# Two transformer layers on one core: order of the work at eight places

## Chip, core and metric

One NeuronCore of a Trainium2 chip (trn2) runs the whole kernel. The metric is the device time of one execution in microseconds (us), as a median over runs. Engines are named as in the profile: PE is TensorE (PEld its weight loads), DVE is VectorE, ACT is ScalarE, POOL is GpSimd, SP is SyncE, which issues most of the DMAs.

## The reference

The input is x of shape [2, 512, 512]: two sequences of 512 tokens with 512 features. Two layers follow one another, each of an attention and a feed-forward part, with a residual addition and a LayerNorm after each part. Cut to what matters:

```python
# layer 0, attention: reads from a memory M (8 heads of 128x128) with a normaliser z
q   = elu(x @ Wq.T + bq) + 1              # only each fourth of 32 heads is used: 8
out = (q @ M) / (q . z + 1e-6)            # per head, repeated four times
x   = layernorm(x + out.reshape(...) @ Wo.T)

# layer 0, feed-forward, quantized: weights in {-1, 0, 1} * scale
xf    = x / 128
inter = silu(xf @ w_gate.T) * (xf @ w_up.T)                 # 1376 wide
iq    = trunc(clip(inter * 128, -128, 127)).astype(int8)
d     = iq @ w_down.T
x     = layernorm(x + trunc(clip(d * 128, -128, 127)))

# layer 1, attention: one head of 128, softmax
q, k, v = split(x @ Wqkv + bqkv)
x = layernorm(x + softmax(q @ k.T / sqrt(128)) @ v @ Wo + bo)

# layer 1, feed-forward in float32
x = layernorm(x + (silu(x @ w_gate.T) * (x @ w_up.T)) @ w_down.T)
```

## The kernel before

The tokens of a sequence are four tiles of 128 rows (t = 0 to 3), the features four blocks of 128 columns (k = 0 to 3), the inner width of the feed-forward parts eleven chunks (c = 0 to 10, the last of 96). x stays on the chip from the first load to the last store, normalised in place. The eight PSUM banks are handed round: a matmul group can begin when the engines that read the bank's earlier content are done.

The order of the work on an engine is that in which the program writes its calls, as far as a scheduler doesn't move an instruction forward; POOL's order is as written. Where the program wants an instruction behind another of the same engine, it says so with `tc.issue_after(step.ins)`. Each engine takes its instructions in that order.

The stages, in order of time:

- Head. `load_x(0)` (L74) issues four loads of x on SP. `rise` (L98) runs nine matmuls on a tile of ones. `transposed` (L105) turns x on PE, a block k per bank, and copies each bank to SBUF, even blocks on ACT (L124), odd ones on DVE (L126). `queries(b, xt, h)` (L318) multiplies by Wq and applies elu + 1: two ACT passes, one on DVE (L331).
- The four parts of Wo of a head are summed by `sum_weights` on DVE or POOL (L345, L347), and `fold` multiplies them into the memory. The buffers of Wo are six, so SP can issue a later load only when an earlier tile was summed. `largest` (L169, L174) takes the maximum of the gate and up weights, from which their scale follows; `check_up` compares each chunk with its ternary form on ACT (L398) and DVE.
- Attention reads. `read(b, t, ...)` (L357) does eight matmuls per tile (L366) and adds the results to x on DVE (L388) and, for three heads, through ACT and POOL; `norm_a0` normalises the tile of the read before. After the seventh read (i = 6), `split(0)` (L249) turns sequence 0 into four blocks and cuts each into a high part (ACT, L259) and a low part (DVE, L260), all four in a row.
- Up projection of layer 0. `up(b, c)` (L515) does 32 matmuls (L522) into two banks, silu on ACT (L535), the product, the cut and the int8 parts on DVE and ACT. The order is `up(0, 0..2)`, `split(1)`, `up(1, 0..2)`, then both sequences by turns. `to_divide` names the ternary weights that ACT makes after each call. `check_down` (L561) compares w_down with its ternary form, through POOL (L400).
- Down projection of layer 0. `f0_down(i)` (L605) starts tile i (22 matmuls, L575), reads it out (`scaled`, L592), adds the tile before (`added`) with its LayerNorm statistics (L132, L134, and POOL's root, L140 and L141), and normalises the one before that (`layernorm_apply`, L146), which is tied behind the last addition of the tile before. Two tiles are started before `up(1, 10)`, the last of the up projection.
- Layer 1, attention. `scores(b)` (L777) makes four banks of scores and, for each, the row maximum (L784, L785) in the same loop; `exponentials` (L789) follows. `values`, `output` and `attended` follow. `norm_a1(b, t)` (L856) takes statistics, then POOL makes the root and the offset (L140 to L842), then ACT applies it (L843).
- Layer 1, feed-forward. Each operand is split into three parts, so that each product is three fast matmuls. `split_rows(b, room)` (L873) does this for x: transposes (L879), a copy (L885), a cut and `row_parts`. `up1` multiplies (L937) and adds up (`sum_up`, L947 and L948). `down1(b, t, got, cuts)` (L1000) does the down projection and the last LayerNorm; the last tile runs in two halves of 256 columns (`cuts` = 2), whose normalisations stand behind one another on DVE (L146), with one store on SP and one on ACT (L1033).

Of the kernel before, what the change touches and what calls it, by code (L numbers as in the profile page):

```python
# [36 lines left out]
def kernel(  # L37
# [36 lines left out]
    def load_x(b):  # L74
        for t in range(NT):
            x = xp.tile([P, HID], F32, tag="x", name=f"x_{b}_{t}")
            nc.sync.dma_start(x, x_in[b, ts(t, P), :])
            xs[b].append(x)
# [19 lines left out]
    rise = psum("rise")  # L98
    for _ in range(9):
        nc.tensor.matmul(rise[:, :P], ones, ones, start=True, stop=True)  # L100
# [3 lines left out]

    def transposed(rows, name, by_tile=False):  # L105

        xt = xtp.tile([P, NK, S], F32, tag="xt", name=f"xt_{name}")
        pts = {}

        def turn(k, t):  # L110
            if k not in pts:
                pts[k] = psum(f"pt_{name}_{k}")
            nc.tensor.transpose(pts[k][:, ts(t, P)], rows[t][:, ts(k, P)], ident)

        if by_tile:
            for t in range(NT):
                for k in range(NK):
                    turn(k, t)
        for k in range(NK):
            if not by_tile:  # L120
                for t in range(NT):
                    turn(k, t)
            if k % 2 == 0:
                copies.append(nc.scalar.copy(xt[:, k, :], pts[k]))  # L124
            else:
                copies.append(nc.vector.tensor_copy(xt[:, k, :], pts[k]))  # L126
        return xt

    def layernorm_stats(row, name):

        st = small.tile([P, 6], F32, tag="st", name=f"st_{name}")
        nc.vector.bn_stats(st, row)  # L132
        mv = small.tile([P, 2], F32, tag="mv", name=f"mv_{name}", bufs=8)
        nc.vector.bn_aggr(mv, st)  # L134
        return root(mv, name)
# [113 lines left out]
    def split(b):  # L249

        hi = xtp.tile([P, NK, S], F32, tag="xt", name=f"xh_{b}").bitcast(F32R)
        los = [pair_tile(f"xl_{b}_{i}").bitcast(F32R) for i in range(2)]
        his = [hi[:, k, :] for k in range(NK)]
        los = [los[k // 2][:, k % 2, :] for k in range(NK)]
        for k in range(NK):
            pt = psum(f"pt_f0{b}_{k}")
            for t in range(NT):
                nc.tensor.transpose(pt[:, ts(t, P)], xs[b][t][:, ts(k, P)], ident)
            nc.scalar.copy(his[k], pt)  # L259
            nc.vector.tensor_sub(los[k], pt, his[k].bitcast(F32))  # L260
        return his + los

# [11 lines left out]
    with tc.tile_pool(name="a0w", bufs=1) as a0w, tc.tile_pool(name="a0", bufs=2) as a0:  # L274
# [42 lines left out]

        def queries(b, xt, h):  # L318

            pq = psum(f"pq_{b}_{h}")  # L320
            for k in range(NK):
                nc.tensor.matmul(  # L322
                    pq, wq[h][:, k, :], xt[:, k, :], start=(k == 0), stop=(k == NK - 1)
                )

# [91 lines left out]
        qs = [[], []]  # L417
        xt = transposed(xs[0], "a00", by_tile=True)
        for h in range(NH):
            queries(0, xt, h)  # L420
            if h == 4:
# [55 lines left out]
        for i, (b, t) in enumerate(order):  # L477
# [7 lines left out]
            if i in (3, 4, 5):  # L485
                for a in range(2):
                    divided(i - 3, a)
            elif i == 6:
                x2.append(split(0))
        norm_a0(len(order) - 1, steps)  # L490
# [16 lines left out]
    with tc.tile_pool(name="f0", bufs=2) as f0:  # L507
# [6 lines left out]

        def up(b, c):  # L515
            n = CHUNKS[c][1]
# [17 lines left out]
            sg = fp.tile([P, S], F32, tag="sg", name=f"sg_f0{b}_{c}")  # L534
            nc.scalar.activation(sg[:n], pp[0][:n], AF.Silu, scale=silu_scale[:n])  # L535
            y = f0.tile([P, S], F32, tag="y", name=f"y_f0{b}_{c}")
# [50 lines left out]

        pds, ys, stats, behind = {}, {}, {}, {}

        def scaled(i):  # L590
            y = f0.tile([P, HID], F32, tag="y", name=f"yd_{i}")
            nc.scalar.activation(y, pds[i], AF.Copy, scale=down_scale)  # L592
            cut_to_12(y)
            ys[i] = y

        def added(i):
# [4 lines left out]
            nc.vector.scalar_tensor_tensor(x, tb, 128.0, x, ALU.min, ALU.subtract)  # L601
            behind[i] = nc.vector.scalar_tensor_tensor(x, x, -1.0, ta, ALU.mult, ALU.add)
            stats[i] = layernorm_stats(x, f"f0_{i}")

        def f0_down(i):  # L605
# [5 lines left out]
            if 0 <= i - 2 < len(order):  # L611

                b, t = order[i - 2]
                with tc.issue_after(behind[min(i, len(order)) - 1].ins):
                    layernorm_apply(xs[b][t], xs[b][t], stats[i - 2])

        for c in range(3):
            up(0, c)
        x2.append(split(1))
        to_divide.insert(2, None)  # L620
        for c in range(3):
            up(1, c)
        for c in range(3, 8):
            step = up(0, c)
            if c == 3:
                with tc.issue_after(step.ins):
                    mx_d = largest([wds[0]], "down")
            elif c == 4:
                sc_d, inv_d = scales(top_d, "down")
            up(1, c)  # L630
            if c == 3:
                top_d = over_partitions(mx_d, "down")
            else:
                for i in range(2 * c - 8, 2 * c - 6):
                    check_down(i)
        up(0, 8)
        check_down(8)
        check_down(9)
# [10 lines left out]
        for i in range(2):  # L649
            f0_down(i)  # L650
        up(1, 10)
        for i in range(2, len(order) - 1):
# [123 lines left out]

    def scores(b):  # L777
        qt, kt, _ = qkv[b]
        got = []
        for t in range(NT):  # L780
            p = psum(f"psc_{b}_{t}")
            nc.tensor.matmul(p, qt[:, ts(t, P)], kt, start=True, stop=True)
            mx = small.tile([P, 1], F32, tag="mx", name=f"mx_{b}_{t}", bufs=8)
            nc.vector.reduce_max(mx, p, AX.X)  # L784
            scaled_max = nc.vector.tensor_scalar_mul(mx, mx, -scale)  # L785
            got.append((p, mx))
        return got, scaled_max

# [16 lines left out]

    got, scaled_max = scores(0)
    got1, scaled_max = scores(1)
    exponentials(0, got)
    for b in range(B):
        for t in range(NT):  # L810
            nc.gpsimd.tensor_add(xs[b][t], xs[b][t], bo)
    pt0 = transposed(probs[0][0], "p0")
    table(AF.Silu, exponentials(1, got1, {1: copies[-4], 2: copies[-2]}))
    with tc.issue_after(scaled_max.ins):
# [58 lines left out]
    def split_rows(b, room):  # L873

        parts, moved = [], []
        for k in range(NK):
# [3 lines left out]
            if b or k:  # L880
# [5 lines left out]
                pt = rows  # L886
            m = cut(pt, S, f"x{b}_{k}")
            parts.append(room[3 * k : 3 * k + 3])
# [14 lines left out]
    x3[0], done = split_rows(0, rooms[0])  # L903
    with tc.issue_after(done.ins):
        for t in range(NT):
            norm_a1(1, t)

# [92 lines left out]
    def down1(b, t, got, cuts):  # L1000
# [22 lines left out]
        nc.vector.bn_aggr(mv, st)  # L1023
        stats = root(mv, f"f1_{b}_{t}")
        if cuts == 1:
            scalar_norm(x, stats, f"f1_{b}_{t}")
            nc.sync.dma_start(out[b, ts(t, P), :], x)
        else:
            for i in range(cuts):
                cols = slice(i * w, (i + 1) * w)  # L1030
                layernorm_apply(x[:, cols], x[:, cols], stats)
                eng = nc.scalar if i else nc.sync
# [92 lines left out]
```

## Time and profile before

| | |
|---|---|
| Median of 3 runs | 488.73 us (488.49 to 488.89) |
| The profiled execution's own time | 488.72 us |
| Its span in the trace | 486.9 us |
| Mean granted TensorE clock | 0.997 |
| PE busy / idle in the span | 473.4 / 13.5 us |
| First matmul of the warm-up, first transpose | 1.16, 5.16 us |
| First query matmul | 8.13 us |
| End of statistics of the last tile, last issue of a store | 482.4, 484.1 us |

How to read it: the span runs from the first to the last recorded instruction; the profiled execution's own time is 1.8 us longer. A line of the timeline has the start and the length in us, the engine, the line of the program, the operation, output and inputs, their shapes, and how many instructions are merged into it; in brackets stands how long the engine was idle before it, and which instruction of which engine ended that. A matmul's end is modelled, so the starts say more than the ends. A float32 matmul has two records.

### The profile page before, as it was taken

The page shows a single profiled execution, that of the slowest core. Times are in us where ns is not written, and L with a number is a line of the kernel's source. Part 1 is how long each engine was busy: PE and PEld are TensorE (multiplying, and loading weights), DVE is VectorE, ACT ScalarE, POOL GpSimd, SP SyncE. Part 2 cuts the span into 40 slices and gives each one's busy share as a digit, 9 for nine tenths or more (in the row PEclk, how much of TensorE's full clock was granted, in tenths as well). Part 3 has the DMA queues.
Part 4 walks back from the last instruction along what each step waited for, and adds up shares of the span by engine and source line. Part 5 has one row for each costly group of instructions (what it writes and reads, how often), then busy time and mean ns, then how long its engine had stood idle before and what let it go on. Part 6 is the DMA issues. An engine that isn't in the chain of part 4 may idle for free.

```text
span 486.9 us, 5812 instructions
## 1 busy us (share of the span) xinstructions
PE 473.4 (97%) x1885; PEld 328.6 (67%) x1885; DVE 352.9 (72%) x682; ACT 275.0 (56%) x513; POOL 115.2 (24%) x155
## 2 busy tenths in 40 slices
PE   8999999999999999999899999999999999999995
PEld 6454444434487788787666467788788888888885
DVE  1456677677675477754989989698876687999942
ACT  2344799555767666545835845776754566333310
POOL 0334102666520096000347032100000000023211
PEclk9999999999999999999999999999999999999998
DMA  8989800000052001131390000000000000000111
GB/s 295 389 314 339 319 1 1 0 0 1 2 160 74 1 3 45 45 90 34 119 370 4 1 0 2 0 2 0 1 0 0 1 1 1 0 22 24 43 45 43
DMA packets 13749, 33.99 MB, mean 70 GB/s; under 512 B 1872, under 2 KB 2768, under 8 KB 13712
## 3 DMA queue, kind: packets, MB, share of 16 engines
q1 hardware_dynamic: 13568, 33.37, 19.3%
q8 instruction: 22, 0.36, 0.3%
q14 instruction: 15, 0.12, 0.1%
q10 hardware_dynamic: 144, 0.13, 0.1%
HBM read 31.40 MB, written 2.10 MB: 69 GB/s over the span
## 4 chain that ended last, share of the span: by engine, by line
PE 58%; DVE 15%; ACT 8%; issue 4%; POOL 2%; POOLq 0%; DVEq 0%; ACTq 0%
PE pm L937 15%; PE pdm L1012 8%; PE pg_f L522 8%; PE pu_f L522 8%; PE pc L937 8%; PE pdc L1012 4%; DVE x L388 4%; ACT y L379 2%; ACT t L398 2%; PE po L847 1%; PE pot L830 1%; PE po L366 1%; DVE x L146 1%; PE pd_f L575 1%; DVE mx L784 1%
## 5 line engine op out<-in xcount | busy, mean ns | idle before, releaser
L366 PE MATMUL po<-mw,q 128*128 128x512 f32 x128 | 56.7, 597 | 1.2 <-DVE x L388 0.9
L322 PE MATMUL pq<-xt_a,wq 128*128 128x512 f32 x128 | 56.5, 593 | 0.3 <-ACT xt_a L124 0.3
L140 POOL TENSOR_TENSOR rstd_f<-mv_f,ln_eps 128x1 f32<-128x1 f32 x16 | 4.5, 283 | 193.3 <-DVE mv_f L1023 139.1
L366 PEld LDWEIGHTS po<-mw,q 128*128 128x128 f32 x128 | 23.2, 189 | 33.2 <-issue 18.9
L322 PEld LDWEIGHTS pq<-xt_a,wq 128*128 128x128 f32 x128 | 24.0, 190 | 29.6 <-issue 28.1
L937 PE MATMUL pm<-r,it_early 128*128 128x512 f32 x144 | 37.7, 392 | 0.4 <-ACT r L695 0.4
L937 PE MATMUL pm<-r,ugu 128*128 128x512 f32 (+1 forms) x144 | 36.8, 393 | 0.0
L937 PEld LDWEIGHTS pm<-r,it_early 128*128 128x128 f32 x144 | 26.9, 188 | 6.6 <-ACT r L695 0.7
L388 DVE SCALAR_TENSOR_TENSOR x<-po,den,x 128x511 f32<-128x511 f32 x40 | 29.8, 745 | 2.0
L937 PEld LDWEIGHTS pm<-r,ugu 128*128 128x128 f32 (+1 forms) x144 | 26.8, 186 | 6.3
L162 ACT ACTIVATE ta_f<-y_f,below_half 128x512 int8<-128x512 f32 (+1 forms) x22 | 15.9, 722 | 25.2 <-DVE y_f L152 24.9
L948 DVE SCALAR_TENSOR_TENSOR ev_q<-pm,ev_q 128x512 f32<-128x512 f32 (+1 forms) x28 | 19.2, 688 | 14.3 <-PE pm L937 14.0
L383 POOL TENSOR_TENSOR y<-y,y 128x511 f32<-128x511 f32 x16 | 20.3, 1270 | 32.1 <-ACT y L379 31.4
L400 POOL TENSOR_SCALAR td<-wd,inv_down 128x512 fp32r<-128x512 f32 (+1 forms) x11 | 19.5, 1790 | 30.3 <-DVE inv_down L196 30.3
L937 PE MATMUL pc<-r,ugu 128*128 128x512 f32 (+1 forms) x96 | 26.1, 394 | 0.0
L545 DVE SCALAR_TENSOR_TENSOR it_f<-tb_f,ta_f 128x512 fp32r<-128x512 int16 (+1 forms) x22 | 15.1, 688 | 15.1 <-ACT tb_f L163 15.1
L327 ACT ACTIVATE e<-pq,bq 128x512 f32<-128x512 f32 x16 | 11.1, 693 | 25.9 <-PE pq L322 25.9
L522 PE MATMUL pg_f<-xh,tu 128*128 128x512 f32 (+1 forms) x88 | 25.6, 406 | 0.1
L522 PE MATMUL pg_f<-xl,tu 128*128 128x512 f32 (+1 forms) x88 | 24.4, 395 | 0.1
L522 PE MATMUL pu_f<-xh,tu 128*128 128x512 f32 (+1 forms) x88 | 24.0, 394 | 0.0
L331 DVE SCALAR_TENSOR_TENSOR q<-e,r 128x512 f32<-128x512 f32 x16 | 13.8, 862 | 13.9 <-ACT r L329 13.9
L522 PE MATMUL pu_f<-xl,tu 128*128 128x512 f32 (+1 forms) x88 | 23.9, 393 | 0.0
(286 smaller groups left out, 1114.9 us busy)
## 6 DMA issues: line engine op xcount, KB each, us to landing
gu<-in_gu SPq DMA_DIRECT2D x20, 512.0 KB, 8.9
wo<-in_wo SPq DMA_DIRECT2D x16, 512.0 KB, 7.4
wd<-in_wd SPq DMA_DIRECT2D x20, 256.0 KB, 4.8
x<-in_x SPq DMA_DIRECT2D x8, 256.0 KB, 4.6
wq<-in_wq SPq DMA_DIRECT2D x8, 256.0 KB, 4.6
out<-x SPq DMA_DIRECT2D x7, 256.0 KB, 2.0
gu<-in_gu SPq DMA_DIRECT2D x2, 384.0 KB, 6.5
wqkv<-in_wqkv SPq DMA_DIRECT2D x1, 768.0 KB, 10.7
```

What stands on the lines that cost most here:

```text
L162: nc.scalar.activation(a[:n], y, AF.Relu, bias=below_half[:n])
L322: nc.tensor.matmul(pq, wq[h][:, k, :], xt[:, k, :], start=(k == 0), stop=(k == NK - 1))
L331: nc.vector.scalar_tensor_tensor(q, e, 1.0, r, ALU.min, ALU.add)
L366: nc.tensor.matmul(po, qs[b][h0 + j][:, ts(t, P)], mw[:, h0 + j, :], start=True, stop=True,)
L383: nc.gpsimd.tensor_add(ys[0][:, :LAST], ys[0][:, :LAST], y[:, :LAST])
L388: steps.append(nc.vector.scalar_tensor_tensor(x[:, :LAST], four[j][:, :LAST], d, x[:, :LAST], ALU.mult, ALU.add))
L400: eng.tensor_scalar(out, w, factor, None, ALU.mult)
L522: nc.tensor.matmul(pp[a][:n], t[:, a, i % NK, :n], x2[b][i], start=(i == 0), stop=(i == 2 * NK - 1),)
L545: nc.vector.scalar_tensor_tensor(it[:n], tb[:n], 128.0, ta[:n], ALU.min, ALU.subtract)
L937: nc.tensor.matmul(p[:n], w, x, start=(left[id(p)] == begun[id(p)]), stop=(left[id(p)] == 1))
L948: nc.vector.scalar_tensor_tensor(ev[:n], pm, MAIN, ev[:n], ALU.mult, ALU.add)
L1012: nc.tensor.matmul(p[:, :w], got[j // 4][1][kind][:n, j % 4], down_parts[j][kind][:, cols], start=(j == 0 and kind == kinds[0]), stop=(j = ...
```

## The change

Eight places are changed. (1) The four loads of sequence 0 go to SP and ACT by turns, the warm-up has eight matmuls, and the first transposes, their copies and the first query run in two halves of 256 tokens. (2) Two of the four blocks of `split(0)` follow the sixth read, two the seventh. (3) In the up projection, `up(0, 3)` follows the split of sequence 1, and sequence 0 stays a chunk further ahead. (4) The last silu is tied behind the read-out of the first two down tiles, and a tile's normalisation is tied behind the first statistics instruction of the next tile instead of behind its addition. (5) The last row maximum of sequence 1 stands behind a copy of the turned probabilities. (6) A cut of sequence 0's second block is tied behind the first block's last part. (7) The normalisation of sequence 1 after attention takes all four statistics first and applies on DVE. (8) In the last tile, the mean is subtracted on DVE beside the root on POOL, and the halves are multiplied by the root on DVE and ACT.

```diff
     def load_x(b):
...
-            nc.sync.dma_start(x, x_in[b, ts(t, P), :])
+            eng = nc.scalar if b == 0 and t % 2 else nc.sync
+            eng.dma_start(x, x_in[b, ts(t, P), :])
...
-    for _ in range(9):
+    for _ in range(8):
         nc.tensor.matmul(rise[:, :P], ones, ones, start=True, stop=True)
...
-    def transposed(rows, name, by_tile=False):
+    def transposed(rows, name, cuts=0):
...
+        def copy(k, at, i=0):
+            move = nc.vector.tensor_copy if k % 2 else nc.scalar.copy
+            copies.append(move(xt[:, k, at], pts[k, i][:, at]))
+
+        if cuts:
+            for i in range(cuts):
+                for t in range(i * NT // cuts, (i + 1) * NT // cuts):
+                    for k in range(NK):
+                        turn(k, t, i)
                 for k in range(NK):
-                    turn(k, t)
...
+                    copy(k, ts(i, S // cuts), i)
...
+    taken = {}
+
     def layernorm_stats(row, name):
...
-        nc.vector.bn_stats(st, row)
+        taken[name] = nc.vector.bn_stats(st, row)
...
     def split(b):
...
-        for k in range(NK):
+
+        def block(k):
             pt = psum(f"pt_f0{b}_{k}")
...
-        return his + los
+
+        return his + los, block
...
-        def queries(b, xt, h):
+        def queries(b, xt, h, cuts=1):
...
+            for i in range(cuts):
+                at = ts(i, S // cuts)
+                for k in range(NK):
+                    nc.tensor.matmul(
+                        pq[:, at], wq[h][:, k, :], xt[:, k, at],
+                        start=(k == 0), stop=(k == NK - 1),
+                    )
...
-        xt = transposed(xs[0], "a00", by_tile=True)
+        xt = transposed(xs[0], "a00", cuts=2)
         for h in range(NH):
-            queries(0, xt, h)
+            queries(0, xt, h, 1 if h else 2)
...
-            elif i == 6:
-                x2.append(split(0))
+            if i == 5:
+                parts, block = split(0)
+                x2.append(parts)
+            if i in (5, 6):
+                for k in range(2):
+                    block(2 * (i - 5) + k)
...
-        def up(b, c):
+        def up(b, c, behind=()):
...
-            nc.scalar.activation(sg[:n], pp[0][:n], AF.Silu, scale=silu_scale[:n])
+            with ExitStack() as tied:
+                for step in behind:
+                    tied.enter_context(tc.issue_after(step.ins))
+                nc.scalar.activation(sg[:n], pp[0][:n], AF.Silu, scale=silu_scale[:n])
...
-            nc.scalar.activation(y, pds[i], AF.Copy, scale=down_scale)
+            moved[i] = nc.scalar.activation(y, pds[i], AF.Copy, scale=down_scale)
...
-                with tc.issue_after(behind[min(i, len(order)) - 1].ins):
+                with tc.issue_after(taken[f"f0_{min(i, len(order)) - 1}"].ins):
                     layernorm_apply(xs[b][t], xs[b][t], stats[i - 2])
 
+        to_divide[2:2] = [None, None]
         for c in range(3):
             up(0, c)
-        x2.append(split(1))
-        to_divide.insert(2, None)
+        parts, block = split(1)
+        x2.append(parts)
+        for k in range(NK):
+            block(k)
+        step = up(0, 3)
+        with tc.issue_after(step.ins):
+            mx_d = largest([wds[0]], "down")
         for c in range(3):
             up(1, c)
-        for c in range(3, 8):
-            step = up(0, c)
-            if c == 3:
-                with tc.issue_after(step.ins):
-                    mx_d = largest([wds[0]], "down")
-            elif c == 4:
+        top_d = over_partitions(mx_d, "down")
+        for c in range(4, 8):
+            up(0, c)
+            if c == 4:
                 sc_d, inv_d = scales(top_d, "down")
-            up(1, c)
-            if c == 3:
-                top_d = over_partitions(mx_d, "down")
-            else:
-                for i in range(2 * c - 8, 2 * c - 6):
-                    check_down(i)
+            up(1, c - 1)
+            for i in range(2 * c - 8, 2 * c - 6):
+                check_down(i)
         up(0, 8)
+        up(1, 7)
         check_down(8)
...
-        up(1, 10)
+
+        up(1, 10, moved.values())
...
     def scores(b):
...
-            nc.vector.reduce_max(mx, p, AX.X)
-            scaled_max = nc.vector.tensor_scalar_mul(mx, mx, -scale)
-            got.append((p, mx))
-        return got, scaled_max
+            got.append((p, small.tile([P, 1], F32, tag="mx", name=f"mx_{b}_{t}", bufs=8)))
+
+        def maxima(tiles):
+            for t in tiles:
+                p, mx = got[t]
+                nc.vector.reduce_max(mx, p, AX.X)
+                done = nc.vector.tensor_scalar_mul(mx, mx, -scale)
+            return done
+
+        return got, maxima
...
-    got, scaled_max = scores(0)
-    got1, scaled_max = scores(1)
+    got, maxima = scores(0)
+    maxima(range(NT))
+    got1, maxima = scores(1)
+    maxima(range(NT - 1))
...
     pt0 = transposed(probs[0][0], "p0")
+    with tc.issue_after(copies[-3].ins):
+        scaled_max = maxima([NT - 1])
...
-            m = cut(pt, S, f"x{b}_{k}")
+            with ExitStack() as tied:
+                if b == 0 and k == 1:
+                    tied.enter_context(tc.issue_after(done.ins))
+                m = cut(pt, S, f"x{b}_{k}")
...
-    with tc.issue_after(done.ins):
-        for t in range(NT):
-            norm_a1(1, t)
+    stats1 = []
+    for t in range(NT):
+        with tc.issue_after(done.ins):
+            stats1.append(layernorm_stats(xs[1][t], f"a11_{t}"))
+    for t in range(NT):
+        with tc.issue_after(taken["a11_3"].ins):
+            layernorm_apply(xs[1][t], xs[1][t], stats1[t])
...
-        stats = root(mv, f"f1_{b}_{t}")
...
         else:
+            rstd = small.tile([P, 1], F32, tag="rstd", name=f"rstd_f1_{b}_{t}", bufs=8)
+            nc.vector.tensor_scalar(rstd, mv[:, 1:2], LN_EPS, None, ALU.add)
+            nc.gpsimd.tensor_tensor(rstd, rstd, minus_half, ALU.pow)
+            nc.vector.tensor_scalar(x, x, mv[:, 0:1], None, ALU.subtract)
+            nc.vector.tensor_scalar(x[:, :w], x[:, :w], rstd, None, ALU.mult)
+            nc.scalar.activation(x[:, w:], x[:, w:], AF.Copy, scale=rstd)
             for i in range(cuts):
                 cols = slice(i * w, (i + 1) * w)
-                layernorm_apply(x[:, cols], x[:, cols], stats)
```

## The prediction

> **What bounds the kernel now.** I read the busy table first, then the idle time of TensorE (PE) in the timeline, wherever one of its lines carries a wait. Here is the page's table and the chain that ended last:
>
> ```profile
> PE 473.4 (97%) x1885; PEld 328.6 (67%) x1885; DVE 352.9 (72%) x682; ACT 275.0 (56%) x513; POOL 115.2 (24%) x155
> PE 58%; DVE 15%; ACT 8%; issue 4%; POOL 2%; POOLq 0%; DVEq 0%; ACTq 0%
> ```
>
> PE is busy for 473.4 of 486.9 us, so only 13.5 us are idle, and the change removes no matmul but one. All it can win is PE's waits, its start and what follows its last matmul. The waits of the timeline (start, us, engine and line, operation; in brackets the idle time and who ended it):
>
> ```profile
> 8.13 2.41 PE L322 MATMUL pq<-xt_a,wq 128*128 128x512 f32 x5 [0.35 <-ACT xt_a L124]
> 125.46 1.12 PE L366 MATMUL po<-mw,q 128*128 128x512 f32 x2 [0.87 <-DVE x L388]
> 145.97 0.19 PEld L522 LDWEIGHTS pg_f<-xh,tu 128*128 128x128 f32 x1 [0.29 <-ACT xh L259]
> 222.35 0.69 ACT L535 ACTIVATE sg_f<-pg_f,silu_scale 96x512 f32<-96x512 f32 x1 [3.74 <-PE pg_f L522]
> 242.38 0.66 PE L113 MATMUL pt_a<-ident,x 128*128 128x128 f32 x4 [1.55 <-DVE x L146]
> 255.22 1.53 PE L113 MATMUL pt_a<-ident,x 128*128 128x128 f32 x12 [0.80 <-DVE x L146]
> 277.27 1.55 PE L830 MATMUL pot<-xt_p,v 128*128 128x512 f32 x3 [0.49 <-DVE xt_p L126]
> 307.51 1.64 PE L879 MATMUL pt_f<-ident,x 128*128 128x128 f32 x13 [1.04 <-ACT x L843]
> ```
>
> A matmul's recorded end reaches beyond the start of the next, so idle time understates a wait. I price a wait as start less previous start, less the usual step: 0.43 us (fp32, 512 columns), 0.23 (fp32r: eight in 1.86), 0.11 (128-column transpose at full clock). This gives 0.51 us at 8.13, 1.03 at 125.46 and 0.38 at 126.80, 1.77 in eight small pieces from 145.97 to 149.4, 1.71 at 242.38 and 0.51 at 243.38, 0.97 at 255.22, 0.66 at 277.27, 1.24 at 307.51. Together 8.8.
>
> The table by stretches (PE, PEld, DVE, ACT, POOL busy) warns where another engine has no room: ACT is full in 56 to 84, DVE nearly so in 310 to 330.
>
> ```profile
> 56.00:84.00 28.00, 27.93 (x66) 12.16 (x65) 20.26 (x50) 28.00 (x59) 2.53 (x2) 1.00 0.10 35
> 310.00:330.00 20.00, 20.00 (x89) 16.25 (x88) 19.60 (x38) 14.88 (x29) 1.08 (x2) 1.00 0.01 1
> ```
>
> And the end, after PE's last matmul:
>
> ```profile
> 482.46 0.19 POOL L140 TENSOR_TENSOR rstd_f<-mv_f,ln_eps 128x1 f32<-128x1 f32 x1 [5.72 <-DVE mv_f L1023]
> 482.73 0.57 POOL L141 TENSOR_TENSOR rstd_f<-rstd_f,minus_half 128x1 f32<-128x1 f32 x1
> 483.34 0.74 DVE L146 TENSOR_SCALAR x<-x,mv_f,rstd_f 128x256 f32<-128x256 f32 x2 [0.96 <-POOL rstd_f L141]
> 484.10 0.37 ACTq L1033 DMA_DIRECT2D out<-x  x1
> ```
>
> **What the Trainium skill says.** "PSUM — Partial Sum Buffer", section "Engine vs sequencer instructions": ScalarE, VectorE and GpSimdE take their queues strictly first in, first out. The trace agrees: ACT stood idle 3.74 us for the silu at 222.35 while the read-out queued behind it was ready by about 218. "TensorE: Matmul & The Clock Gate", Part 1: the array starts at half clock and gets full clock after about 3.4 us of steady work, in a free-running window. Here transposes step 0.21 us until 6.62 and 0.11 after, 5.5 us after the first matmul: longer, same pattern. "SBUF — State Buffer", section "SBUF: two separate sides": DVE and GpSimd share a port pair that one locks for an instruction. It agrees: a normalisation on DVE (L146) takes 0.55 us at 241.78 and 1.49 at 253.68, beside POOL's additions of bo. "DMA: Bandwidth & Descriptors", section "Issuing engines are not separate DMA queues": a second issuer saves only issue time. The first four loads of x take 1.81 us to issue on SP.
>
> **The change, part by part.** Times are those of before.
>
> 1. Head. One warm-up matmul less is two records of 0.213: transposes begin at 4.73, not 5.16. Eight of 16 are done by about 6.6. Their four half copies, two each on ACT and DVE, lie beside the other eight, which end at about 7.4. A 128x256 copy isn't in the trace; it lies between half and all of 0.59/0.69, and I take 0.4 (L1018 takes 0.42 for 256 columns from PSUM). First query matmul at about 7.5 instead of 8.13: -0.6. The second halves are needed 0.86 later and are ready. Two x loads go to ACT's queue, ahead of a table load nobody waits for. Cost: on DVE the addition of wo1 now precedes a query, and SP's later wo and gu loads slip by up to 0.6; two maxima of gu (1.26 us, they wait for gu_0, which landed at 36.5) now stand ahead of both DVE copies of sequence 1's transposes. I get these at 38.5 and 39.7 against needs of 38.6 and 40.3. Taken: -0.6; from -0.75 to +0.5.
>
> 2. First split in halves. Two of its four blocks go one read earlier, so ACT's copy and DVE's subtraction (2 us each in a row before) no longer stand between one read's banks and the next. Of 1.03+0.38 about 0.4 stays, since the second pair still meets the last read: -1.0; from -1.5 to -0.2.
>
> 3. First sequence ahead in the up projection. The chunk (0,3) lies between the split of sequence 1 and its use: 3.7 us of matmuls over 2.04 of ACT copies and 2.7 of DVE. The 1.77 goes, except about 0.45 while a last block's copy waits in ACT's queue behind that chunk's silu: -1.3; from -1.8 to -0.8. Moved along: the divisions of chunk 3 and after on ACT, two calls later each (still two chunks ahead of use), the maximum of wd_0 (landed 141.6, needed 151), POOL's 11 ternaries of 1.79 (earlier), and SP's loads of the next layer's gate weights (up to 3.7 later at 193, used at 257): free.
>
> 4. Down tiles and normalisation. Read-outs 0 and 1 (0.67 each) move into the 3.74 of idle ACT: the silu waits only if bank 1, full at about 220.4, were late. Each tile costs DVE 0.43+2x0.69+0.68+0.17+0.54=3.2 us against PE's 2.57, so DVE lags; statistics ahead of the preceding apply remove the waits for POOL's root (0.44, 0.44, 0.56, 0.71, 0.76). Walking both queues: x3 is applied at 240.6 rather than 242.33, PE wants it at 240.8. ACT must still do three read-out steps before it copies the transposes, so the query starts at 242.45 against 243.38: -0.93. x7 is applied at 251, not 255.17, and PE wants it at 253: -0.97. Taken -1.9; from -2.7 to -0.9 (the second only, if ACT's order decides the first).
>
> 5. Last maximum of sequence 1 (0.68+0.15) behind the copy: 0.66+0.1 goes; the exponential, Silu table (1.28) and ot copy run about 0.4 later, of which PE sees 0.2: -0.5; from -0.75 to 0.
>
> 6. Cut of k1 behind k0's third part: k3, which ends the chain, ends as before: 0; from -0.35 to 0.
>
> 7. Second normalisation. Four statistics first, then applies on DVE: four ACT passes of 0.81 and two POOL steps each go, 4x0.54=2.2 of DVE are added where DVE stood idle 3.84 us (304.2 to 308.0). x3 is ready at 305.3, PE asks at 305.9: -1.2. If that cover were gone, the rows' split in 310 to 330 (19.6 of 20 busy) would be late by up to 2.2-1.2. From -1.24 to +1.
>
> 8. End. eps on DVE (about 0.15, as L785) for POOL's 0.19+latency, mean subtracted during the root, then half on DVE and half on ACT together instead of 0.37+0.37. A 128x256 multiply on ACT isn't shown: between 0.37 and 0.69, I take 0.4. Last issue 483.7 instead of 484.1: -0.4; from -0.45 to 0.
>
> Sum: -0.6-1.0-1.3-1.9-0.5-1.2-0.4 = -6.9. The profiled execution took 488.72 (span 486.9 plus 1.8 around it), the median of the runs is 488.73, so no correction: 481.8.
>
> **Rivals.** (a) Part is given back: DVE is the limit. For: 3.2 against 2.57 per down tile, 19.6 of 20 in 310 to 330. Against: DVE is idle 3.84 just before 308. Then part 4 wins 0.95, part 7 0.2, parts 2 and 3 0.6 and 1.0, part 8 0.3, parts 1 and 5 as taken: -4.1, 484.6. (b) Nearly every wait goes: the good ends of the parts sum to 9.5; without part 6 (0.35) and with part 3's 0.45 left: -8.7, 480.0. For: each waiter has another engine's idle time beside it. Against: in-order ACT. (c) Slower: DVE waits at L174 for gu_0 in front of sequence 1's copies. PE is late by the landing less 36.5; slower than before if gu_0 lands after 43.4. For: SP's loads are chained to wo buffers that DVE and POOL free. Against: I find a slip of 0.6. At a landing at 45: 490.4. That the readouts do not move ahead of the silu would cost part 4's half and falls under (a).
>
> **Chances.** Forecast 0.52 (480.9 to 483.3), (a) 0.23, (b) 0.12, (c) 0.10, no measurable difference 0.03. The bound for that is 0.2%, about 1 us, what a measurement of this kernel can tell. Faster 0.87, same 0.03, slower 0.10. The range 479.5 to 486.0 leaves out (c), no difference and the far ends of (a) and (b).
>
> **What would show it.** In the profile after: first query at 7.5; no wait over 0.5 at the last read and the first up of sequence 1; ACT reading pd_0 before the last silu; transposes after the down stage waiting under 0.2 for x and the second group not at all; no wait of PE at L879; the two last issues within 0.15 us. Wrong, if DVE waits at L174 with PE idle before sequence 1's first queries, or if the rows' split after 310 ends later than PE's need.

## The result, and the profile after

The changed kernel takes 482.03 us (median of 4 runs, 481.09 to 482.17) against 488.77 for the kernel before; the ratio is 0.9859, with a 95% interval of 0.9842 to 0.9876. The forecast was 481.8. The profiled execution took 481.89, with a span of 479.7.

The page's first row and the chain that ended last, of the kernel after:

```profile
PE 470.9 (98%) x1891; PEld 329.6 (69%) x1891; DVE 349.9 (73%) x689; ACT 272.5 (57%) x512; POOL 115.1 (24%) x146
PE 71%; ACT 7%; DVE 5%; issue 3%; POOL 1%; POOLq 0%; DVEq 0%; ACTq 0%
```

DVE's share of the chain fell from 15% to 5%, and PE's grew from 58% to 71%: PE now leads the work over more of the span. The timeline of the kernel after, at the places that were shown of before (lines of the program have moved by up to 44):

```profile
7.21 2.11 PE L334 MATMUL pq<-xt_a,wq 128*128 128x256 f32 x9
118.61 4.53 PE L379 MATMUL po<-mw,q 128*128 128x512 f32 x10 [0.21 <-DVE mv_a L142]
147.54 1.42 PE L539 MATMUL pg_f<-xh,tu 128*128 128x512 f32 x4
217.17 0.69 ACT L612 ACTIVATE yd<-pd_f,down_scale 128x512 f32<-128x512 f32 x1 [1.32 <-PE pd_f L595]
218.99 0.67 ACT L555 ACTIVATE sg_f<-pg_f,silu_scale 96x512 f32<-96x512 f32 x1
239.17 2.41 PE L778 MATMUL pqk<-xt_a,wqkv 128*128 128x512 f32 x5 [1.04 <-ACT xt_a L119]
249.71 1.91 PE L115 MATMUL pt_a<-ident,x 128*128 128x128 f32 x16
270.51 3.60 PE L863 MATMUL pot<-xt_p,v 128*128 128x512 f32 x8
299.86 1.91 PE L912 MATMUL pt_f<-ident,x 128*128 128x128 f32 x16
```

Where PE had a bracket before there is none now, or a shorter one; the sixteen transposes at 249.71 and at 299.86 run in one row. One large wait is left, 1.04 at 239.17, where the first query of layer 1 waits for ACT's copy of the turned x. A part of it stood there before, behind the longer wait for DVE's normalisation:

```profile
243.38 1.55 PE L755 MATMUL pqk<-xt_a,wqkv 128*128 128x512 f32 x3 [0.35 <-ACT xt_a L124]
```

From start to start, less the usual step, it was 0.51 and is now 1.21. A wait of 0.41 idle at 288.42, in the split of layer 1's rows, also stood there before (at 294.34); the prediction's list of waits had left it out.

Matching PE's matmuls by name in both traces and taking after less before shows where the time came from (us, at the start of the matmul named):

| up to | cumulative | of this part | forecast |
|---|---|---|---|
| 1: queries of sequence 0 | -1.00 | -1.00 | -0.6 |
| 2: first up chunk | -1.86 | -0.86 | -1.0 |
| 3: first down tile | -3.32 | -1.46 | -1.3 |
| 4: queries of layer 1, both sequences | -5.24 | -1.92 | -1.9 |
| 5: last output of sequence 1 | -5.92 | -0.68 | -0.5 |
| 6 and 7: after sequence 1's transposes; PE's last matmul | -7.30 | -1.38 | -1.2 |
| 8: last issue of a store | -7.44 | -0.14 | -0.4 |
| last store landed | -7.29 | +0.15 | |
| the execution's own time | -6.83 | +0.46 | |

The sum came out at 6.83 against 6.9, but not by its parts: up to its last matmul PE gained 0.8 more than forecast (7.30 against 6.5), and the end gave back 0.47 where 0.4 was to be won. That the two nearly cancel is luck.

### The profile page after: what moved, and what is told of

The parts are those of the page before. It is cut to its first block, busy times and chain, and to the rows that moved or that the text cites. A ratio compares the mean times of both kernels' runs of the same rounds, so it can differ in the third digit from the quotient of the medians.

```text
span 479.7 us, 5815 instructions
## 1 busy us (share of the span) xinstructions
PE 470.9 (98%) x1891; PEld 329.6 (69%) x1891; DVE 349.9 (73%) x689; ACT 272.5 (57%) x512; POOL 115.1 (24%) x146
## 4 chain that ended last, share of the span: by engine, by line
PE 71%; ACT 7%; DVE 5%; issue 3%; POOL 1%; POOLq 0%; DVEq 0%; ACTq 0%
PE pm L977 17%; PE pg_f L539 9%; PE pc L977 9%; PE pu_f L539 9%; PE pdm L1052 7%; PE pd_f L595 4%; PE pdc L1052 4%; DVE x L401 4%; PE pqk L778 3%; PE po L379 2%; ACT y L392 2%; ACT t L411 2%; PE pv L791 1%; PE po L880 1%; PE pot L863 1%
## 5 line engine op out<-in xcount | busy, mean ns | idle before, releaser
L334 PE MATMUL pq<-xt_a,wq 128*128 128x512 f32 (+1 forms) x136 | 56.4, 567 | 0.0
L334 PEld LDWEIGHTS pq<-xt_a,wq 128*128 128x128 f32 x136 | 25.5, 190 | 27.5 <-issue 25.5
L987 ACT ACTIVATE ev_q<-pc 128x512 f32<-128x512 f32 (+1 forms) x28 | 16.4, 591 | 12.1 <-PE pc L977 12.1
```

What stands on the lines that cost most here:

```text
L334: nc.tensor.matmul(pq[:, at], wq[h][:, k, :], xt[:, k, at], start=(k == 0), stop=(k == NK - 1),)
L987: nc.scalar.activation(ev[:n], pc, AF.Copy, scale=CROSS)
```

## The experiments

Each is one edit to the changed kernel, the last joins two of them. Part 5 has no experiment of its own. The moment at which PE gets its full clock at the start differed between runs (below), so a loss is taken from PE's last matmul less the first query (466.42 us in the changed kernel), where nothing else is said. Medians are of 4 runs (5 for the last).

**The loads of x on one queue.**

```diff
-            eng = nc.scalar if b == 0 and t % 2 else nc.sync
-            eng.dma_start(x, x_in[b, ts(t, P), :])
+            nc.sync.dma_start(x, x_in[b, ts(t, P), :])
```

> The changed kernel, with the four first loads of x all issued by SP, as before. Two theories. A (the gain of the head comes from one warm-up matmul less and from half copies, not from the second queue): the first query starts at 7.2 to 7.3 us as in the changed kernel, PE's last matmul at 473.6, so the span stays at 479.7 within 0.2. B (the second queue is needed, since x lands later from one queue): x's last tile lands at 6.2 instead of 5.5, its transposes wait, and the first query starts 0.5 or more later; the span grows by 0.5. Beside that an open point: the time around the span grew from 1.8 us before to 2.2 us after the change. If the loads on ACT's queue cause it, it falls back to 1.8 here, and the time is 481.5; if they don't, it stays at 2.2 and the time is 481.9.

Measured: median 482.09, span 479.8, first query at 7.32. Theory A holds: in this trace, with the full clock at 6.1 (6.2 in the changed kernel), the second queue is worth 0.1 to 0.2. The last tile of x landed at 6.54 instead of 5.46, just ahead of its transposes at 6.7; with an earlier full clock it would be missed sooner, but no run shows that. The time around the span stays at 2.2, so these loads don't cause it.

**The end as before.**

```diff
-            rstd = small.tile([P, 1], F32, tag="rstd", name=f"rstd_f1_{b}_{t}", bufs=8)
...
+            stats = root(mv, f"f1_{b}_{t}")
             for i in range(cuts):
                 cols = slice(i * w, (i + 1) * w)
+                layernorm_apply(x[:, cols], x[:, cols], stats)
```

> The changed kernel, with the last tile's normalisation as before (eps and root on POOL, both halves on DVE one after the other). The prediction's part 8: the last issue of a store comes 0.4 later than in the changed kernel, the span grows by 0.4 to 480.1. Rival, from the trace of the changed kernel: only 0.14 us lie between the two ends, and the store on ACT landed 0.15 later after its issue than before, so the span grows by less than 0.15.

Measured: median 481.79. From PE's last matmul to the last issue it is 3.17 us, against 3.03 in the changed kernel; to the last landing 4.95 against 4.98. The span grew by more (480.2), but 0.24 of that was there before the end. The rival holds: the new end is worth 0.14 at the issue and nothing at the landing.

**ACT subtracts for its half.**

```diff
-            nc.vector.tensor_scalar(x, x, mv[:, 0:1], None, ALU.subtract)
-            nc.vector.tensor_scalar(x[:, :w], x[:, :w], rstd, None, ALU.mult)
+            less = small.tile([P, 1], F32, tag="off", name=f"less_{b}_{t}")
+            nc.vector.tensor_scalar(less, mv[:, 0:1], -1.0, None, ALU.mult)
+            nc.scalar.activation(x[:, w:], x[:, w:], AF.Identity, bias=less)
+            layernorm_apply(x[:, :w], x[:, :w], (mv, rstd))
```

> The changed kernel, but in the last tile ACT subtracts the mean from its own half while POOL takes the root, and DVE does its half in one pass after the root; DVE no longer works on 512 columns beside POOL. Theory A: POOL's root took 0.74 instead of 0.57 because DVE's subtraction held the port that both share; here it takes 0.57 again, and both last issues come 0.1 to 0.2 earlier (span 479.5). Theory B: the root alone takes 0.74 when no addition runs ahead of it on POOL; then the issues move by less than 0.05.

The end in the timeline of the changed kernel, then of this one:

```profile
475.19 0.48 DVE L1071 TENSOR_SCALAR x<-x,mv_f 128x512 f32<-128x512 f32 x1
475.35 0.74 POOL L1070 TENSOR_TENSOR rstd_f<-rstd_f,minus_half 128x1 f32<-128x1 f32 x1 [5.91 <-DVE rstd_f L1069]
476.12 0.51 ACT L1073 ACTIVATE x<-x,rstd_f 128x256 f32<-128x256 f32 x1 [5.82 <-POOL rstd_f L1070]
476.66 0.36 ACTq L1077 DMA_DIRECT2D out<-x  x1
```

```profile
475.47 0.57 POOL L1070 TENSOR_TENSOR rstd_f<-rstd_f,minus_half 128x1 f32<-128x1 f32 x1 [5.91 <-DVE less L1072]
475.48 0.51 ACT L1073 ACTIVATE x<-x,less 128x256 f32<-128x256 f32 x1 [5.07 <-DVE less L1072]
476.08 0.51 ACT L1075 ACTIVATE x<-x,rstd_f 128x256 f32<-128x256 f32 x1
476.62 0.35 ACTq L1079 DMA_DIRECT2D out<-x  x1
```

POOL's root takes 0.57 with DVE off the tile and 0.74 beside DVE's 512 columns: theory A. (It takes 0.57 in the kernel with the old end too, where DVE stands idle.) From PE's last matmul to the last issue it is 2.87 instead of 3.03, to the landing 4.87 instead of 4.98. Median 481.47.

This trace also says something on part 1. The head is the changed kernel's, but the full clock came at 6.7 instead of 6.2, so the same sixteen transposes took longer (2.88 instead of 2.64) and the queries start at 7.44 instead of 7.21:

```profile
4.73 2.88 PE L115 MATMUL pt_a<-ident,x 128*128 128x128 f32 x16
7.44 4.91 PE L334 MATMUL pq<-xt_a,wq 128*128 128x256 f32 x19
```

**ACT's copy first.**

```diff
             b, t = order[i]
-            ta, tb = truncated_parts(f0, ys[i], P, f"d{i}")
+            with ExitStack() as tied:
+                if i == len(order) - 2:
+                    tied.enter_context(tc.issue_after(copies[-2].ins))
+                ta, tb = truncated_parts(f0, ys[i], P, f"d{i}")
```

> The changed kernel, with ACT's two int8 and int16 parts of the seventh down tile tied behind ACT's copies of sequence 0's transposes. In the changed kernel PE waits 1.2 us there (first attention query at 239.17), for ACT, which does these two parts first. Theory A: PE's wait is ACT's order alone, since DVE reaches the seventh tile's addition only at 240.6: the query starts at about 238.5, everything after comes 0.7 earlier, span 479.0. Theory B (DVE is the limit in this stage): the later parts delay the last two tiles, the transposes of sequence 1 wait instead, and the span stays within 0.2 of 479.7.

ACT and PE around the wait at 239.17, in the changed kernel and then in this one:

```profile
237.32 0.71 ACT L171 ACTIVATE tb_d<-yd,below_half 128x512 int16<-128x512 f32 x1
237.93 0.71 ACT L170 ACTIVATE ta_d<-yd,below_half 128x512 int8<-128x512 f32 x1
238.55 1.06 ACT L119 COPY xt_a<-pt_a 128x512 f32<-128x512 f32 x2
```

```profile
237.35 1.07 ACT L119 COPY xt_a<-pt_a 128x512 f32<-128x512 f32 x2 [0.41 <-PE pt_a L115]
237.99 1.55 PE L781 MATMUL pqk<-xt_a,wqkv 128*128 128x512 f32 x3 [0.35 <-ACT xt_a L119]
```

The first query starts 1.18 earlier; 0.48 of this was there before, at the end of the up projection, so the edit gives 0.70, and it stays to the end: theory A. Median 481.05 (480.66 to 483.17: one of the four runs was 2.1 above the median, and no trace of it was kept). At this query ACT's order was the limit in the changed kernel, not DVE.

**The head in one piece.**

```diff
-        xt = transposed(xs[0], "a00", cuts=2)
+        xt = transposed(xs[0], "a00", cuts=1)
...
-            queries(0, xt, h, 1 if h else 2)
+            queries(0, xt, h, 1)
```

> The changed kernel, with the first transposes, their copies and the first query in one piece of 512 tokens again (eight warm-up matmuls and both queues kept). Theory (the prediction's part 1, mended by the trace): the half copies hide the copy that PE waited for; without them PE waits 0.5 us for ACT's first copy again, as before at 8.13, and the first query starts about 0.5 after the last transpose instead of 0.1. Rival: the gain of the head was the earlier loads and one warm-up matmul less; then the first query moves by less than 0.2. The moment at which the full clock comes differs from run to run by up to 0.7 us at the head, so the wait is read from the trace, not from the span.

```profile
7.21 1.07 ACT L119 COPY xt_a<-pt_a 128x512 f32<-128x512 f32 x2 [4.28 <-PE pt_a L115]
7.84 1.55 PE L334 MATMUL pq<-xt_a,wq 128*128 128x512 f32 x3 [0.35 <-ACT xt_a L119]
```

The wait is back, 0.51 by start to start, as at 8.13 before: the first query comes 0.62 after the last transpose, instead of 0.11. The theory holds. Median 482.03, the same as the changed kernel's: a loss of half a us does not show there.

**The first split in one piece.**

```diff
-            if i == 5:
+            elif i == 6:
                 parts, block = split(0)
                 x2.append(parts)
-            if i in (5, 6):
-                for k in range(2):
-                    block(2 * (i - 5) + k)
+                for k in range(NK):
+                    block(k)
```

> The changed kernel, with the four blocks of sequence 0's split all behind the seventh read again. Theory: the parts are independent, PE's waits of 1.03 and 0.38 at the last read are back, and from there to the end everything is 0.85 later than in the changed kernel (the change's trace shows 0.86 gained there). Rival (other waits take it back): the up projection behind it has room, so less than 0.4 remains at PE's last matmul.

```profile
124.98 1.12 PE L379 MATMUL po<-mw,q 128*128 128x512 f32 x2 [0.86 <-DVE x L401]
126.32 3.24 PE L379 MATMUL po<-mw,q 128*128 128x512 f32 x7 [0.22 <-DVE mv_a L142]
```

Both waits are back, 1.03 and 0.38 by start to start, and PE's last matmul is 0.80 later. The theory holds. Median 482.35.

**The up projection by turns.** The edit restores the old loop of the change's diff.

```diff
-        to_divide[2:2] = [None, None]
...
+        to_divide.insert(2, None)
         for c in range(3):
             up(1, c)
-        top_d = over_partitions(mx_d, "down")
-        for c in range(4, 8):
+        for c in range(3, 8):
...
```

> The changed kernel, with the old order of the up projection (sequence 1's first chunks straight behind its split). Theory: the eight small waits, 1.77 in all, are back, PE is 1.46 later at the end of the up projection and at its last matmul. Rival: the head start of the chunks also relieves the stage after it; then the loss at PE's last matmul differs from that at the end of the up projection by more than 0.3.

The transposes, ACT's cast and the first matmul that waits for it, in the kernel before and then in this one:

```profile
144.01 1.91 PE L258 MATMUL pt_f<-ident,x 128*128 128x128 f32 x16
145.35 2.04 ACT L259 CAST xh<-pt_f 128x512 fp32r<-128x512 f32 x4
```

```profile
141.56 1.91 PE L267 MATMUL pt_f<-ident,x 128*128 128x128 f32 x16
143.65 2.04 ACT L268 CAST xh<-pt_f 128x512 fp32r<-128x512 f32 x4
144.28 1.96 PE L539 MATMUL pg_f<-xh,tu 128*128 128x512 f32 x4 [0.80 <-ACT xh L268]
```

Measured: 2.27 lost at the end of the up projection and 2.20 at PE's last matmul; median 484.09. This is more than the 1.46 that the change gained there, so the theory has the place right and the size wrong; the two losses differ by less than 0.3, so the rival fell. The first of the eight waits is 0.97 here and was 0.22 before; the others are as before. In the kernel before, ACT's cast began 1.34 after the transposes did (145.35 less 144.01), here 2.09 after (143.65 less 141.56). The reading of the two traces: part 2 had moved PE forward, but not ACT's queue, so without part 3 this wait takes 0.75 of part 2's 0.86 back. No kernel has both parts undone, so this is argued, not shown.

**The last silu not tied.**

```diff
-        up(1, 10, moved.values())
+        up(1, 10)
```

> The changed kernel, without the tie of the last silu: ACT takes the silu before the read-outs of the first two down tiles. The prediction's part 4: ACT idles 3 us or more for that silu again, DVE begins its down work some 3 us later, and since DVE needs 3.2 us per tile against PE's 2.57, the lateness reaches the transposes of sequence 0: PE loses 0.5 to 1.2 there and 0.3 to 1.0 at sequence 1's. Rival: the order of statistics and applications brought the whole gain, and the two read-outs catch up within the eight tiles: less than 0.2 lost at PE's last matmul.

ACT idles 3.74 again, and x of sequence 0 is late by 1.7 again:

```profile
238.59 0.66 PE L115 MATMUL pt_a<-ident,x 128*128 128x128 f32 x4 [1.54 <-DVE x L154]
```

The table by stretches shows something more. A line has the stretch and its length, the busy time of PE, PEld, DVE, ACT and POOL, then PE's granted clock, the DMA share and GB/s:

```profile
236.00:239.00 3.00, 1.46 (x13) 1.21 (x11) 3.00 (x7) 1.95 (x4) 0.91 (x2) 1.00 0.90 281
239.00:243.00 4.00, 3.65 (x7) 1.51 (x6) 3.90 (x9) 2.15 (x4) 1.59 (x4) 0.57 0.95 329
243.00:250.00 7.00, 7.00 (x30) 4.08 (x29) 5.65 (x11) 2.48 (x4) 4.32 (x6) 1.00 1.03 358
```

After PE had been half idle for 3 us, its granted clock fell to half for 3.4 us (0.57 as a mean from 239 to 243); matmuls lasted 1.06 instead of 0.61. From the end of the up projection to PE's last matmul 2.59 is lost, of which 0.89 stood at the first query and 1.64 came by the last query of sequence 1, with the fallen clock. The four runs took 482.44, 482.69, 484.0 and 484.2 (median 483.34). One trace was kept, of the run of 484.0. The granted clock, a mean over the run, was 0.993 in both long runs and 0.996 and 0.997 in the short ones, so the other long run very likely lost its clock too. So the theory's direction and its 0.5 to 1.2 at the first group hold, and the rival fell; what the missing tie costs at sequence 1's transposes can't be read beside the fallen clock, which was in no theory.

**Normalisation ahead of the statistics.**

```diff
-            nc.vector.scalar_tensor_tensor(x, x, -1.0, ta, ALU.mult, ALU.add)
+            added_last[i] = nc.vector.scalar_tensor_tensor(x, x, -1.0, ta, ALU.mult, ALU.add)
...
-                with tc.issue_after(taken[f"f0_{min(i, len(order)) - 1}"].ins):
+                with tc.issue_after(added_last[min(i, len(order)) - 1].ins):
```

> The changed kernel, with a tile's normalisation in the down stage tied behind the last addition of the next tile again, ahead of its statistics; the silu stays behind the two read-outs. The prediction's part 4: DVE waits 0.4 to 0.8 for POOL's root at each late tile, and PE loses up to 0.9 at the two groups of transposes together. Rival: with the early read-outs DVE is ahead anyway and the root is ready in time; less than 0.2 lost at PE's last matmul.

```profile
250.16 1.09 PE L115 MATMUL pt_a<-ident,x 128*128 128x128 f32 x8 [0.35 <-DVE x L154]
276.16 1.13 PE L880 MATMUL po<-wo,ot 128*128 128x512 f32 x2
```

Nothing is lost at sequence 0's query, 0.52 at sequence 1's transposes, and 0.33 more at 276.16, where PE waits for a copy on ACT; 0.87 at PE's last matmul. Median 482.52. The prediction's size holds (up to 0.9), but half of it comes where none was foreseen: nothing at the first group, and a part behind the second.

**The second cut not tied.**

```diff
-            with ExitStack() as tied:
-                if b == 0 and k == 1:
-                    tied.enter_context(tc.issue_after(done.ins))
-                m = cut(pt, S, f"x{b}_{k}")
+            m = cut(pt, S, f"x{b}_{k}")
```

> The changed kernel, without the tie of sequence 0's second cut behind the first block's third part. The prediction's part 6: nothing at PE's last matmul, since the fourth block's part ends as before. Rival, from the trace: PE's second wait in the split's stage was 0.44 before and 0.24 after the change, so 0.2 is lost and stays.

The matmul that waits, in the changed kernel and then in this one:

```profile
289.22 0.50 PE L977 MATMUL pc<-r,it_early 128*128 128x512 f32 x1
```

```profile
289.63 0.50 PE L974 MATMUL pc<-r,it_early 128*128 128x512 f32 x1 [0.28 <-DVE r L720]
```

PE's wait is 0.44 instead of 0.23, and from 294.4 on nothing of it is left: 0.01 at the last matmul. The prediction holds, the rival fell; median 481.84.

**Sequence 1's normalisation on ACT.**

```diff
-    stats1 = []
-    for t in range(NT):
-        with tc.issue_after(done.ins):
-            stats1.append(layernorm_stats(xs[1][t], f"a11_{t}"))
-    for t in range(NT):
-        with tc.issue_after(taken["a11_3"].ins):
-            layernorm_apply(xs[1][t], xs[1][t], stats1[t])
+    with tc.issue_after(done.ins):
+        for t in range(NT):
+            norm_a1(1, t)
```

> The changed kernel, with sequence 1's normalisation after attention one tile at a time and applied on ACT, as before. Theory (part 7): PE waits 1.24 for the last tile at the transposes of sequence 1 again, and is 1.17 later to the end. Rival: DVE, freed of 2.2 us of applications, catches up in the rows' split that follows and PE gets some of it back: less than 0.8 at the last matmul.

```profile
300.73 0.33 PE L912 MATMUL pt_f<-ident,x 128*128 128x128 f32 x1 [0.24 <-ACT x L876]
302.10 1.09 PE L912 MATMUL pt_f<-ident,x 128*128 128x128 f32 x8 [1.04 <-ACT x L876]
```

Two waits, 0.40 and 1.26, and 1.58 lost at PE's last matmul; nothing of it comes back behind, so the rival fell. The loss is above the 1.17 of the theory: the wait of 0.40 had no match before. Median 483.00, which is only 0.97 more than the changed kernel's: here the time around the span is 1.8 again (2.2 in the changed kernel). One line of the profile page differs in the same way, here in the changed kernel and then in this one:

```profile
q14 instruction: 14, 0.11, 0.1%
```

```profile
q14 instruction: 15, 0.12, 0.1%
```

It counts the transfers of instructions on queue 14 within the span; the kernel before has 15 too.

**The two that won, together.**

```diff
+                    tied.enter_context(tc.issue_after(copies[-2].ins))
...
+            nc.scalar.activation(x[:, w:], x[:, w:], AF.Identity, bias=less)
+            layernorm_apply(x[:, :w], x[:, :w], (mv, rstd))
```

The edit is those of the copy-first kernel and of the one in which ACT subtracts.

> Both versions that won in the trace together: the changed kernel, with ACT's parts of the seventh down tile behind its copies, and with ACT subtracting the mean of its own half in the last tile. Theory: the parts are independent: 0.70 at the first attention query and 0.1 to 0.16 at the last stores, so 0.8 less than the changed kernel, about 481.2 as a median. Rival: the two don't add up, or the differing moment of the full clock (up to 0.7 us) hides them: a median within 0.3 of 482.0.

Median 480.55 (480.18 to 481.52); ratio to the kernel before 0.983, interval 0.9817 to 0.9844. It has the lowest median of all, and the first query of layer 1 is 0.70 earlier relative to the end of the up projection, as in the copy-first kernel; the end is that of the kernel in which ACT subtracts (2.87 to the last issue). So in the trace the two add up, as the theory says. The median is 1.5 below the changed kernel's, more than the theory's 0.8; with a spread of 1.3 between runs the rest is not explained. In the profiled run, the slowest of the five, the third rival of the prediction showed itself:

```profile
36.65 1.28 DVE L182 TENSOR_REDUCE mx_up<-gu 128x1 f32<-128x512 f32 x2 [1.95 <-DMA gu<-in_gu]
37.85 0.68 DVE L119 COPY xt_a<-pt_a 128x512 f32<-128x512 f32 x1
38.58 1.98 PE L334 MATMUL pq<-xt_a,wq 128*128 128x512 f32 x4 [1.06 <-DVE xt_a L119]
```

PE had its full clock by 4.1 us and started its queries 0.9 earlier than in the changed kernel's trace, but DVE waited for gu_0 with the copies of sequence 1 behind it, and PE lost 1.22. The early clock was given back, and more.

## Why the prediction was right

It was right in its frame: PE bounds the kernel, and each wait removed moves the rest. Parts 2 to 5 and 7 came within 0.2 of their terms, and taking 2, 3, 4 and 7 away, each alone, made PE's last matmul later (0.80, 2.20, 2.92 and 0.87 for the two edits of part 4, 1.58); the 2.92 has the fallen clock in it. For part 5 only the table speaks. By its steps:

- Part 1 measured 1.00 against 0.6, and about half of the difference is luck. The warm-up matmul that is gone is two records of 0.213, and the transposes did begin 0.43 earlier. But in this trace the full clock also came earlier, at 6.22 instead of 6.62. Had it come at the same moment, the two records less would have counted at the full clock's step, 0.22, and not 0.43. The kernel in which ACT subtracts has the same head, got its full clock at 6.7, and starts its queries at 7.44, where the prediction said 7.5. So the mechanism was right: 0.22 for the warm-up matmul and 0.51 for the wait. Another 0.1 is what a wait costs the next record, which the pricing didn't count.
- Part 3 took 3.7 us of matmuls as the cover, and that is right: the program writes a chunk's 32 matmuls in two branches of 16, and one of them runs.
- Part 4's total was right, its two halves too (0.90 and 1.02 against 0.93 and 0.97), and so was its warning that ACT's order would leave a wait: 1.2 us at 239.17, of which the copy-first kernel wins 0.70. The prediction didn't say which of the two edits brings which half. Without the tie of the silu 0.89 is lost by the first query; without the order of statistics nothing is lost there, but 0.52 at the second group and 0.33 behind it.
- Parts 2 and 3 were priced as if independent. By the two traces they are not: with part 3 undone, 0.75 of part 2's gain goes into a longer first wait. Their sum holds since both were made.
- Part 8 was too large: 0.14 instead of 0.4 at the issue. A multiply of 256 columns took 0.51 on ACT (0.4 was taken), and POOL's root took 0.74 instead of 0.57, since DVE's subtraction ran beside it. "SBUF — State Buffer", section "SBUF: two separate sides", which the prediction had cited for the other direction, says that the one that comes second is blocked. The kernel in which ACT subtracts agrees in direction. In size the trace shows less than a full block: the subtraction ran on for 0.32 after the root had begun (475.35 to 475.67), and the root took only 0.17 longer; times of such short POOL instructions are rough.
- The time around the span was taken as fixed at 1.8, and it is 2.2. From the last landing to the end, span and surroundings together, before took 2.82, the changed kernel 3.28. Of the twelve kernels only the one with part 7 undone is back at 2.83, the others take 3.23 to 3.30; in the kernel with the old end the rest stands between two entries of POOL's queue, behind the last landing (0.39 instead of 0.08). So it comes with part 7 and takes some 0.45 of that part's gain. The transfers of instructions on queue 14 go along with it. Before and with part 7 undone the span holds 15 of them, and the last starts about 17 us ahead of the last landing. In all twelve other traces it holds 14, and the next one starts 1.9 to 2.3 us behind the last landing. Those two kernels also have the most instructions on POOL, 155 and 154; the others have 146 or 147. This points to an instruction transfer that now falls into the ending. No experiment changed the number of POOL's instructions alone, so the cause stays open.
- Rival (a) fell: behind 300 no wait of PE is above 0.1, though DVE is busy for 19.86 of 20 us from 303 to 323. Rival (b), nearly every wait gone and 480.0, was not reached: PE still waited 1.2 at 239.17. Rival (c) is real but small: in two of fourteen traces PE waited there (0.23 and 1.22), both times because the full clock came early (4.0 and 4.1), not because gu_0 was late (it landed between 34.7 and 37.1 in all, and at 37.1 PE didn't wait).

## What to carry to other kernels

Price a PE wait by start to start, undo the parts one by one, and compare at a late matmul of the trace: medians that spread over 1 us could not have told 0.2 from 0.8. Two removed waits in a row are not two gains: the first moves PE towards the second's producer, so walk that producer's queue again from the new time. Work taken away ahead of the full clock is worth its time at full speed, unless the clock moves too: compare heads of the program only between runs that got the clock at the same moment. An instruction that waits for a load should not stand on an in-order engine ahead of copies that PE needs soon.

## What the runs showed of the hardware

- The full clock came at a different moment in each trace: by the granted clock, and by the step of the matmuls (0.213 to 0.109 us), between 4.0 and 7.3 us over fourteen traces, 2.8 to 6.2 after the first matmul, though PE worked without a pause from that matmul on. "TensorE: Matmul & The Clock Gate", Part 1, says that the window runs freely; its half a us to either side is too narrow here. In the twelve kernels whose first copies run in halves, the first query started between 6.3 and 7.8. The spread between runs of one kernel is about 1 us too, but one trace for each kernel can't show that it comes from there; an early clock can also be given back, as in the last kernel.
- A gap of 1.54 us in PE, in a stretch of 3 us that was half idle, was followed by half the clock for 3.4 us once (the silu kernel; by the mean clock of 0.993 probably in two of its four runs). A like gap of 1.55 us in the kernel before was not.
- The record behind one that waited starts about 0.10 late as well (0.53 instead of 0.43 at 239.17 and at 276.16). A float32 matmul has two records.
